# A DiT attention block: the first round of fp32 score products of each step in tiles of 32 rows by 64 columns

## The chip, the core and the metric

The program runs on one core of a Trainium2 chip. The metric is the device time of one execution in microseconds (us), as a median of several runs. Lower is better.

## The reference

One transformer block with adaptive layer norms, in fp32: x is 2 x 2048 x 576, there are 16 heads of 36 features, and every weight and product is fp32.

```python
qkv = (xn @ w_qkv + b_qkv).reshape(B, N, 3, H, hd)
q, k, v = (qkv[:, :, 0], qkv[:, :, 1], qkv[:, :, 2])
q = _ln(q, 1e-05, qn_g, qn_b)
k = _ln(k, 1e-05, kn_g, kn_b)
attn = jnp.einsum('bqhd,bkhd->bhqk', q, k) * scale
attn = jax.nn.softmax(attn, axis=-1)
o = jnp.einsum('bhqk,bkhd->bqhd', attn, v).reshape(B, N, C)
```

Ahead of it stand the modulated layer norm of x, behind it the output projection, a residual, a second norm and a GELU MLP of width 2304. The change touches only the line with `q, k`.

## The kernel before

The block is worked batch by batch: rows are normed and multiplied with w_qkv, then `attend` works the attention of the whole batch, then come projection and MLP. All order on TensorE is the order in which the kernel's text issues the products (a manual schedule).

`attend` walks over steps (p, qb, g): a pair of heads p (8 pairs), a block of 512 queries qb (4 blocks), and a quarter g of the keys (4 quarters). That is 128 steps for a batch and 256 in all. A step issues two things to TensorE:

- `scores(p, qb, g)`: two rounds, one for each `k0`. A round fills four PSUM banks, one for each row group of 32 rows: a row group holds one head of the pair and one half of the keys. In each bank stand 128 keys (partitions) by 512 queries. First the 32 main features are multiplied, in fp32, out of `km` and `qm` (four products of 32 rows by 128 columns, one for each row group); then the remaining four features are added out of `ke` and `qe`, as 16 rows of fp32r parts (again four products, at 128 columns). ScalarE then takes the exponential of each bank into a `pt` tile (L1540).
- `values` of the step before (L1549): the exponentials, 128 rows, against 64 columns of `vt`, in two column tiles, one for each head of the pair, which stand in the two halves of one bank. Four `pt` tiles and two heads make eight products.

So TensorE goes in each step from 32-row tiles of 128 columns (scores) to 128-row tiles of 64 columns (values) and back. The kernel has eight banks; a step takes nine of them in turn (eight for scores, one for values). Every product reads its stationary operand by a weight load (shown as PEld) and then streams 512 columns. An fp32 product is shown as two loads and two matmuls, an fp32r product as one of each.

Two other places come up in the prediction. L178 multiplies the modulation's rows in four column tiles of 32 columns, at 128 rows and then at 64. L1714 and L1717 are the output projection, in tiles of 64 rows and of 128 rows by 128 columns.

Of the kernel before, what the change touches and what calls it, by code (L numbers as in the profile page):

```python
# [16 lines left out]
P = 128  # L17
# [10 lines left out]
DIMS = 32  # L28
# [3 lines left out]
def dit_block(  # L32
# [25 lines left out]
    nc = tc.nc  # L58
    B, N, C = x.shape
    MLP = w1.shape[1]  # L60
    HD = qn_g.shape[0]
# [32 lines left out]
    def bank():  # L94

        return psum["b"].tile([P, 512], F32, tag="b", name="b") if "b" in psum else s_tile()[:, 0, :]
# [650 lines left out]
    def head_rows(first, count=HD):  # L747

        at = first
        while at < first + count:  # L750
            n = min(P - at % P, first + count - at)
            yield at // P, at % P, at - first, n
            at += n

    def block_of_small():
# [108 lines left out]
        def take_k(p):  # L864
            m, e = km[p % 2], ke[p % 2]
            if p > 2:
                not_sooner(m)
                not_sooner(e)
            src = lambda c: slice(c * N // 2, (c + 1) * N // 2)
            rows_taken(nc.gpsimd, m, e, range(2), C + p * 2 * HD, src, slice(0, N // 2))  # L870
            full = slice(0, P)
            return [
                lambda: scaled(m, m, full, 1),
                lambda: parted(e[:, 0:BLK], full, 1),
                lambda: parted(e[:, BLK:], full, 1),
            ]
# [13 lines left out]
        def take_q(p, qb):  # L890
            i, full = qb % 2, slice(0, P)
            src = lambda c: slice(qb * BLK, (qb + 1) * BLK)
            rows_taken(nc.sync, qm[i], qe[i], range(2), p * 2 * HD, src, slice(0, BLK))
            return [lambda: scaled(qm[i], qm[i], full, 0), lambda: parted(qe[i], full, 0)]
# [623 lines left out]
        def attend(b, pool, hooks, key_rows):  # L1518

            def scores(p, qb, g):
                i, j = p % 2, qb % 2
                pts = []
                for k0 in (2 * g * P, (2 * g + 1) * P):
                    keys = slice(k0, k0 + P)
                    banks = [bank() for _ in range(4)]
                    for k, q, first in (  # L1530
                        (km[i], qm[j], True),
                        (ke[i].bitcast(F32R), qe[j].bitcast(F32R), False),
                    ):
                        for r0, ps in zip(range(0, P, 32), banks):
                            r = slice(r0, r0 + (DIMS if first else 4 * (HD - DIMS)))
                            nc.tensor.matmul(ps, k[r, keys], q[r, :], start=first, stop=not first)  # L1536
                    for c in range(2):
                        pt = pool.tile([P, 2, BLK], F32, name="pt", bufs=5)
                        for h in range(2):
                            nc.scalar.activation(pt[:, h, :], banks[2 * c + h], AF.Exp, scale=SCALE)  # L1540
                        pts.append((pt, k0 // P + c * NT // 2))
                return pts

            def values(p, pts):
                acc = bank()
                for pt, kc in pts:
                    for h in range(2):
                        v0 = (kc * H + 2 * p + h) * HV
                        nc.tensor.matmul(  # L1549
                            acc[64 * h : 64 * h + 64, :],  # L1550
                            vt[:, v0 : v0 + 64],
                            pt[:, h, :],
                            start=pt is pts[0][0],
                            stop=pt is pts[-1][0],
                        )
                return acc

            def finish(p, qb, ot, den=None):


                if den is None:
                    den = pool.tile([P, BLK], F32, name="den")
                for h in range(2):
                    sums = den_dram[b, p, qb, h, :]
                    nc.sync.dma_start(out=sums.unsqueeze(0), in_=ot[64 * h + HD : 64 * h + HD + 1, :])
                    nc.sync.dma_start(out=den[64 * h : 64 * h + 64, :], in_=sums.partition_broadcast(64))

                def divided(c0=0, c1=BLK):
                    part = slice(c0, c1)
                    nc.vector.reciprocal(den[:, part], den[:, part])  # L1570
                    nc.vector.tensor_tensor(ot[:, part], ot[:, part], den[:, part], ALU.mult)
                    cols = slice(qb * BLK + c0, qb * BLK + c1)
                    for h in range(2):
                        for c, row, d, n in head_rows((2 * p + h) * HD):
                            for r in (row,) if c < FULL else (row, row + 64):
                                nc.sync.dma_start(
                                    out=held["qo"][r : r + n, c, cols], in_=ot[64 * h + d : 64 * h + d + n, part]
                                )

                return divided  # L1580

            steps = [(p, qb, g) for p in range(NPAIR) for qb in range(NBLK) for g in range(NG)]


            behind, later = None, [[] for _ in range(13)]
            ended = None
            for p, qb, g in [*steps, (None, None, None)]:
                pts = None if p is None else scores(p, qb, g)
                if (p, qb) == (0, 0) and g < len(key_rows):
                    key_rows[g]()  # L1590
                if g == 0 and (p, qb) != (NPAIR - 1, NBLK - 1):
                    for i, do in enumerate(take_q(*((p, qb + 1) if qb + 1 < NBLK else (p + 1, 0)))):
                        later[1 + i].append(do)
                if g == 1 and qb == 0 and p + 1 < NPAIR:
                    for i, do in enumerate(take_k(p + 1)):
                        later[3 + NG * i].append(do)
                if behind is not None:
                    bp, bqb, bg, bpts = behind
                    acc = values(bp, bpts)
                    if bg == 0:  # L1600
                        last = (bp, bqb) == (NPAIR - 1, NBLK - 1)
                        ot = spare[9][:, :BLK] if last else pool.tile([P, BLK], F32, name="ot", bufs=2)
                        nc.vector.tensor_copy(ot, acc)  # L1603
                    else:
                        nc.vector.tensor_tensor(ot, acc, ot, ALU.add)  # L1605
                    if p is None:
                        ended = finish(bp, bqb, ot, spare[10][:, :BLK])
                    elif bg == NG - 1:
                        later[2 if bp == NPAIR - 1 else 3].append(finish(bp, bqb, ot))
                if (p, qb, g) in hooks:  # L1610
                    due = hooks[p, qb, g]() or []
                    later[1] = due[:1] + later[1]
                    later[2] = due[1:] + later[2]
                later.append([])
                for do in later.pop(0):
                    do()
                behind = (p, qb, g, pts)
            for do in [do for group in later for do in group]:
                do()
            return ended  # L1620
# [445 lines left out]
        banks = stack.enter_context(tc.tile_pool(name="ps_m", bufs=1, space=PSUM, reuse_waits="tile"))  # L2066
# [313 lines left out]
        def combined_blocks(out_m, outs):  # L2380

            one = hs.tile([P, QUARTER], F32, name="one", bufs=2)
            nc.scalar.copy(one, out_m[1])  # L2383
            r = hs.tile([P, 2, HALF], F32, name="r", bufs=9)
            left, right = r[:, :, 0:QUARTER], r[:, :, QUARTER:HALF]
            both = lambda ap: ap.unsqueeze(1).to_broadcast([P, 2, QUARTER])
            tt = nc.vector.tensor_tensor
            tt(left, outs[2, 6], both(one), ALU.add)
            tt(right, outs[5, 7], both(left[:, 1]), ALU.add)
            tt(left[:, 1], right[:, 1], out_m[4], ALU.subtract)  # L2390
            tt(right[:, 1], right[:, 1], out_m[5], ALU.add)
            tt(right[:, 0], right[:, 0], out_m[3], ALU.add)
            return r
# [57 lines left out]
        for i, (n, m) in enumerate(products):  # L2451
# [16 lines left out]
            r = combined_blocks(out_m, outs)  # L2468
# [67 lines left out]
```

## Time and profile before

| what | us |
|---|---|
| time, median of 3 runs | 3060.53 (3060.13 to 3061.5) |
| the profiled execution, from its first to its last instruction (its span, and the only time that the profile gives of it) | 3061.8 |
| TensorE busy | 3039.6 (99%) |
| ScalarE busy | 1493.3 (49%) |
| VectorE busy | 1706.3 (56%) |

Busy time is a union of spans in which some instruction of the engine was under way. Matmuls overlap and their ends are modelled, so TensorE at 99% is not TensorE at its peak: the starts of loads and matmuls tell more than their ends.

### The profile page before, as it was taken

The numbers are of one execution on the slowest core, as the hardware profiler recorded it, in microseconds if no ns is written. First come the engines' busy times: TensorE is split into PE (matmuls) and PEld (weight loads), VectorE is DVE, ScalarE is ACT, GpSimd is POOL, SyncE is SP. The second block draws the span as 40 slices with busy tenths as digits, with TensorE's granted clock in tenths as the row PEclk, the third lists the DMA queues.
The fourth block names the chain that finished last, engine by engine and source line by source line (L and its number), as shares of the span: only waits on it lengthen the run. The fifth ranks groups of instructions, "written<-read, shape, count | busy, mean of one in ns | idle before, by whom it ended". The sixth has DMA issues, their size and how long they took to land.

```text
span 3061.8 us, 51356 instructions
## 1 busy us (share of the span) xinstructions
PE 3039.6 (99%) x19015; PEld 1892.7 (62%) x19015; DVE 1706.3 (56%) x2644; ACT 1493.3 (49%) x2917; POOL 1000.6 (33%) x1263
## 2 busy tenths in 40 slices
PE   8999999999999999999999999999999999999998
PEld 6884333333333688633333333347888888999998
DVE  6773455445553666544434444447666664667666
ACT  2326666666666233466666666643555553000000
POOL 4551100132322445201101111115445544545543
PEclk9999999999999999999999999999999999999999
DMA  5773322333333454412222222236888887855554
GB/s 150 187 147 92 103 69 70 81 92 93 94 87 94 162 129 83 94 46 64 52 55 74 62 67 66 77 97 191 250 239 241 243 243 290 311 190 198 206 188 150
DMA packets 427940, 415.17 MB, mean 136 GB/s; under 512 B 231473, under 2 KB 355921, under 8 KB 419553
## 3 DMA queue, kind: packets, MB, share of 16 engines
q1 hardware_dynamic: 390520, 314.46, 34.4%
q0 software_dynamic: 36848, 97.33, 11.7%
q8 instruction: 153, 2.51, 0.3%
q14 instruction: 107, 0.87, 0.1%
q10 hardware_dynamic: 312, 0.01, 0.0%
HBM read 246.43 MB, written 154.75 MB: 131 GB/s over the span
## 4 chain that ended last, share of the span: by engine, by line
PE 99%; DVE 0%; ACT 0%; issue 0%; POOL 0%; DVEq 0%
PE b L1549 30%; PE b L1536 20%; PE b L2366 12%; PE m L2107 12%; PE s L1141 7%; PE s L1227 5%; PE s L1717 4%; PE m L2121 2%; PE one L2107 2%; PE b L2375 2%; PE s L1143 1%; PE s L1233 1%; PE s L1714 1%; PE b L178 0%; PE s L1229 0%; ACT xnt L398 0%
## 5 line engine op out<-in xcount | busy, mean ns | idle before, releaser
L1540 ACT ACTIVATE pt<-b 128x512 f32<-128x512 f32 x2048 | 1057.2, 610 | 482.6 <-PE b L1549 269.4
L1549 PE MATMUL b<-pt,vt 128*64 128x512 f32 x4096 | 935.0, 599 | 0.0
L1549 PEld LDWEIGHTS b<-pt,vt 128*64 128x64 f32 x4096 | 271.9, 136 | 582.0 <-issue 437.6
L1536 PE MATMUL b<-qm,km 32*128 32x512 f32 x4096 | 563.8, 613 | 0.0
L1605 DVE TENSOR_TENSOR ot<-b,ot 128x512 f32<-128x512 f32 x186 | 128.6, 691 | 546.4 <-PE b L1549 546.4
L1536 PE MATMUL b<-qe,ke 16*128 16x512 f32 x2048 | 420.4, 791 | 0.0
L1536 PEld LDWEIGHTS b<-qm,km 32*128 32x128 f32 x4096 | 190.8, 185 | 270.9 <-ACT pt L1540 211.1
L1141 PE MATMUL s<-wq,xnt 128*128 128x288 f32 x864 | 226.7, 406 | 1.5 <-ACT xnt L398 1.5
L2383 ACT COPY one<-b 128x144 f32<-128x144 f32 x55 | 15.3, 278 | 406.0 <-PE b L2366 406.0
L2107 PE MATMUL m<-xnt,wb 128*128 128x256 f32 x864 | 209.1, 379 | 1.4 <-issue 1.3
L2107 PE MATMUL m<-s,wb 128*128 128x256 f32 x864 | 207.4, 379 | 0.0
L1570 DVE RECIPROCAL den<-den 128x512 f32<-128x512 f32 x62 | 206.8, 3336 | 0.0
L1603 DVE COPY ot<-b 128x512 f32<-128x512 f32 x62 | 42.9, 691 | 259.1 <-PE b L1549 253.8
L1141 PEld LDWEIGHTS s<-wq,xnt 128*128 128x128 f32 x864 | 158.0, 190 | 36.9 <-ACT xnt L398 2.2
L1536 PEld LDWEIGHTS b<-qe,ke 16*128 16x128 f32 x2048 | 107.0, 184 | 113.6 <-issue 112.8
L2107 PEld LDWEIGHTS m<-s,wb 128*128 128x128 f32 x864 | 163.6, 190 | 22.0
L2107 PEld LDWEIGHTS m<-xnt,wb 128*128 128x128 f32 x864 | 159.4, 190 | 21.5 <-issue 1.7
L2145 ACT ACTIVATE cs<-cs,b_sb 128x512 f32<-128x512 f32 x144 | 100.1, 720 | 137.8 <-DVE cs L2140 137.6
L1802 POOL DMA_DIRECT2D spare<-in_x_dram x32 | 17.8, 556 | 451.5 <-DVE met L794 451.5
L2147 POOL TENSOR_TENSOR cs<-cs 128x256 f32<-128x256 f32 x72 | 57.5, 798 | 244.5 <-ACT cs L2145 244.5
L1062 ACT ACTIVATE xnt<-xnt,mod 128x128 f32<-128x128 f32 x244 | 100.1, 482 | 51.1 <-DMA xnt<-turned 51.1
L2134 DVE TENSOR_TENSOR cs<-m,cs 128x512 f32<-128x512 f32 x72 | 49.3, 684 | 118.9 <-PE m L2121 76.0
(374 smaller groups left out, 4590.3 us busy)
## 6 DMA issues: line engine op xcount, KB each, us to landing
operands<-cs SPq DMA_DIRECT2D x70, 896.0 KB
wb<-operands SPq DMA_DIRECT2D x37, 1152.0 KB
operand<-operands SPq DMA_DIRECT2D x19, 1152.0 KB
spare<-in_x_dram POOLq DMA_DIRECT2D x64, 288.0 KB, 3.2
x_dram<-spare POOLq DMA_DIRECT2D x64, 288.0 KB, 2.4
qm<-qk SPq DMA_DIRECT2D x256, 64.0 KB
den<-den_dram SPq DMA_DIRECT2D x124, 128.0 KB
spare<-x_dram POOLq DMA_DIRECT2D x37, 288.0 KB, 3.9
```

What stands on the lines that cost most here:

```text
L1062: nc.scalar.activation(part, part, AF.Identity, **affine(which, k, b))
L1141: nc.tensor.matmul(out_a, full[:, k, :], wq[:, k, f], start=k == 0, stop=False)
L1227: nc.tensor.matmul(out[m], x_[:, k, :], w_(k), start=k == 0, stop=k == 1 and m == 6)
L1536: nc.tensor.matmul(ps, k[r, keys], q[r, :], start=first, stop=not first)
L1540: nc.scalar.activation(pt[:, h, :], banks[2 * c + h], AF.Exp, scale=SCALE)
L1549: nc.tensor.matmul(acc[64 * h : 64 * h + 64, :], vt[:, v0 : v0 + 64], pt[:, h, :], start=pt is pts[0][0], stop=pt is pts[-1][0],)
L1570: nc.vector.reciprocal(den[:, part], den[:, part])
L1605: nc.vector.tensor_tensor(ot, acc, ot, ALU.add)
L1717: nc.tensor.matmul(out[m], x_[m][:, k], factors[m][:, k], start=k == 0 and m not in (3, 4), stop=k == 1 and m not in (2, 7),)
L2107: nc.tensor.matmul(out_m[m], wb[:, f, slot[m], k, :], moving[m](k), start=k == 0 and m in firsts, stop=k == 1 and m in lasts,)
L2145: nc.scalar.activation(part, part, AF.Gelu, bias=b1_sb[:, g : g + 1])
L2366: nc.tensor.matmul(out_m[m], stationary[m][:, c, :], w[:, 7 * c + m - 1, :], start=a == 0 and c == 0, stop=ends and c == FULL - 1 and m no ...
```

## The change

In the first round of each step (`k0 == 2 * g * P`) each fp32 product of 32 rows by 128 columns becomes two of 32 rows by 64 columns: first the lower 64 keys of all four row groups, then the upper 64, into the lower and upper 64 partitions of the same four banks. The four fp32r products of that round and the whole second round stay at 128 columns, and so does everything else.

```diff
                 for k0 in (2 * g * P, (2 * g + 1) * P):
-                    keys = slice(k0, k0 + P)
                     banks = [bank() for _ in range(4)]
                     for k, q, first in (
                         (km[i], qm[j], True),
                         (ke[i].bitcast(F32R), qe[j].bitcast(F32R), False),
                     ):
-                        for r0, ps in zip(range(0, P, 32), banks):
-                            r = slice(r0, r0 + (DIMS if first else 4 * (HD - DIMS)))
-                            nc.tensor.matmul(ps, k[r, keys], q[r, :], start=first, stop=not first)
+                        width = 64 if first and k0 == 2 * g * P else P
+                        for c0 in range(0, P, width):
+                            for r0, ps in zip(range(0, P, 32), banks):
+                                r = slice(r0, r0 + (DIMS if first else 4 * (HD - DIMS)))
+                                nc.tensor.matmul(
+                                    ps[c0 : c0 + width, :],
+                                    k[r, k0 + c0 : k0 + c0 + width],
+                                    q[r, :],
+                                    start=first,
+                                    stop=not first,
+                                )
```

## Rows read from the trace of the kernel before

**Rows 1.** The page: busy time of each engine; granted TensorE clock in 40 slices.

```profile
PE 3039.6 (99%) x19015; PEld 1892.7 (62%) x19015; DVE 1706.3 (56%) x2644; ACT 1493.3 (49%) x2917; POOL 1000.6 (33%) x1263
...
PEclk9999999999999999999999999999999999999999
```

**Rows 2.** The chain of waits that ended last: shares of the span by engine and line.

```profile
PE 99%; DVE 0%; ACT 0%; issue 0%; POOL 0%; DVEq 0%
PE b L1549 30%; PE b L1536 20%; PE b L2366 12%; PE m L2107 12%; PE s L1141 7%; PE s L1227 5%; PE s L1717 4%; PE m L2121 2%; PE one L2107 2%; PE b L2375 2%; PE s L1143 1%; PE s L1233 1%; PE s L1714 1%; PE b L178 0%; PE s L1229 0%; ACT xnt L3
```

**Rows 3.** The page's costliest groups: line, operation, tiles, shape, count, busy, mean ns, idle.

```profile
L1540 ACT ACTIVATE pt<-b 128x512 f32<-128x512 f32 x2048 | 1057.2, 610 | 482.6 <-PE b L1549 269.4
L1549 PE MATMUL b<-pt,vt 128*64 128x512 f32 x4096 | 935.0, 599 | 0.0
...
L1536 PE MATMUL b<-qm,km 32*128 32x512 f32 x4096 | 563.8, 613 | 0.0
...
L1536 PE MATMUL b<-qe,ke 16*128 16x512 f32 x2048 | 420.4, 791 | 0.0
L1536 PEld LDWEIGHTS b<-qm,km 32*128 32x128 f32 x4096 | 190.8, 185 | 270.9 <-ACT pt L1540 211.1
```

**Rows 4.** Timeline of weight loads (PEld) over one step: start, length, operation, count, [idle before].

```profile
1307.79 0.31 PEld L1536 LDWEIGHTS b<-qm,km 32*128 32x128 f32 x8 [0.81 <-ACT pt L1540]
1308.32 0.20 PEld L1536 LDWEIGHTS b<-qe,ke 16*128 16x128 f32 x4 [0.22 <-issue]
1308.75 0.45 PEld L1536 LDWEIGHTS b<-qm,km 32*128 32x128 f32 x8 [0.22 <-issue]
1309.42 0.20 PEld L1536 LDWEIGHTS b<-qe,ke 16*128 16x128 f32 x4 [0.22 <-issue]
1310.19 0.20 PEld L1549 LDWEIGHTS b<-pt,vt 128*64 128x64 f32 x4 [0.56 <-ACT pt L1540]
1310.67 0.14 PEld L1549 LDWEIGHTS b<-pt,vt 128*64 128x64 f32 x2 [0.29 <-issue]
1311.10 0.14 PEld L1549 LDWEIGHTS b<-pt,vt 128*64 128x64 f32 x2 [0.28 <-issue]
...
1312.82 0.14 PEld L1549 LDWEIGHTS b<-pt,vt 128*64 128x64 f32 x2 [0.29 <-issue]
1313.77 0.30 PEld L1536 LDWEIGHTS b<-qm,km 32*128 32x128 f32 x7 [0.81 <-ACT pt L1540]
```

**Rows 5.** Timeline of matmuls (PE) of the same step.

```profile
1307.79 1.14 PE L1536 MATMUL b<-qm,km 32*128 32x512 f32 x8
1308.35 0.82 PE L1536 MATMUL b<-qe,ke 16*128 16x512 f32 x4
1308.99 1.04 PE L1536 MATMUL b<-qm,km 32*128 32x512 f32 x8
```

**Rows 6.** Timeline of the projection, where 128-row tiles become 64-row tiles and back.

```profile
2046.81 0.19 PEld L1717 LDWEIGHTS s<-wp,qo 128*128 128x128 f32 x1
...
2047.38 0.30 PEld L1714 LDWEIGHTS s<-wp,qo 64*128 64x128 f32 x4 [0.39 <-DMA spare<-den_dram]
...
2048.22 0.40 PE L1714 MATMUL s<-wp,qo 64*128 64x288 f32 x1
...
2048.55 0.54 PEld L1717 LDWEIGHTS s<-wp_sums,qo 128*128 128x128 f32 x3 [0.39 <-issue]
```

**Rows 7.** Timeline of weight loads where L178's column tiles stand between steps.

```profile
445.72 0.14 PEld L1549 LDWEIGHTS b<-pt,vt 128*64 128x64 f32 x2 [0.28 <-issue]
446.67 0.16 PEld L178 LDWEIGHTS b<-wa,sil 128*32 128x32 f32 x8 [0.81 <-ACT pt L1540]
...
448.96 0.15 PEld L178 LDWEIGHTS b<-wa,sil 64*32 64x32 f32 x8 [0.52 <-issue]
449.63 0.31 PEld L1536 LDWEIGHTS b<-qm,km 32*128 32x128 f32 x8 [0.52 <-issue]
```

**Rows 8.** Timeline of ScalarE over the step of rows 4.

```profile
1309.25 1.08 ACT L1540 ACTIVATE pt<-b 128x512 f32<-128x512 f32 x2 [0.81 <-PE b L1536]
1311.38 3.05 ACT L1540 ACTIVATE pt<-b 128x512 f32<-128x512 f32 x6 [1.04 <-PE b L1549]
```

## The prediction

> **What bounds the kernel now.** First the page: TensorE is busy 99% of the span at full clock in every slice, the other engines a half or less [rows 1]. The chain of waits that ended last says the same: 99% TensorE, 30% of the span in the value products (L1549) and 20% in the score products (L1536) [rows 2]. Whatever TensorE gains or loses per step goes straight into the time. The groups give the counts: 4096 value matmuls at 16 a step are 256 steps, and of a step's 16 fp32 score matmuls (two to a product) the change concerns eight [rows 3].
>
> Busy time can't tell more, since matmuls overlap. The starts of loads and matmuls can: the load of the next pass is issued when a pass begins [rows 4]. One step, from 1307.79 to 1313.77, takes 5.98 us:
>
> - first round: four row groups at once, first fp32 pass 0.53 (1307.79 to 1308.32), second pass 0.43 (to 1308.75), fp32r pass 0.24 (to 1308.99, where the next round's matmuls begin [rows 5]). In all 1.20.
> - second round: 0.43 to 1309.42, another 0.43 and 0.24, which ends at 1310.09; the values begin at 1310.19, 0.10 later.
> - values: first pass 0.48, then 0.43 each. The last load row is at 1312.82, at the start of the seventh of eight passes; two passes on is 1313.68, and the next step begins at 1313.77, 0.09 later [rows 4].
>
> So two things cost TensorE time beside streaming. One is a border of about 0.09 wherever the shape of the tiles changes. The other is the first weight load behind a border, which nothing hides: 0.53 against 0.43 says 0.10 for 128 columns, 0.48 against 0.43 says 0.05 for 64. Inside a mode loads run ahead under the pass before: the second round's first pass takes 0.43 like any other, though its loads are as wide.
>
> The waits put the load at 1313.77 down to ScalarE [rows 4]. I don't believe that: ScalarE is paced by the values, with two exponentials at 1309.25 and six from 1311.38, and ends at 1314.43 [rows 8]. The banks of the first round are old by then, and the idle time is the same 0.81 at a border where another line follows [rows 7]. It is 0.29 + 0.43 + 0.09: the rest of a pass, a pass, the border.
>
> **What the change does to a step.** It removes four fp32 products of 128 columns and adds eight of 64: eight loads and eight matmuls more on TensorE's queue. It adds no transfer, no semaphore wait that another engine has to serve, no bank, no exponential. The product of the streams is the same array work: four row groups by 128 columns before, four row groups by two column halves after. The terms:
>
> 1. *First load.* Values to first round is a border before and after (128*64 to 32*128, now to 32*64). The load behind it has 64 columns in place of 128: 0.05 in place of 0.10, a gain of 0.05. Bounds: 0.05 and nothing (if the two halves of a row group load one after the other). I take 0.05, since two column tiles of 64 columns load together in the values (first pass 0.48 with four loads under way) [rows 4].
> 2. *Eight tiles in place of four.* Loads of one pass start one behind the other: four of 185 ns each [rows 3] span 0.20 [rows 4], so about 6.5 ns apart. The eighth starts 0.045 behind the first. Before, the fp32r pass could follow row group by row group; behind a border it waits for the last tile. Bounds nothing and 0.05; I take 0.05.
> 3. *A new border.* Before, the fp32r products followed in the same mode, 32 rows by 128 columns. Now they come behind tiles of 32*64. The trace has no border from 32*64 to 32*128. It has one where only the rows change, 128*128 to 64*128 and back: a pass of 288 columns is 0.24 (288/512 of 0.43), the last load at 2046.81 and two passes make 2047.29, and the next tile begins at 2047.38; back, 2048.22 and one pass is 2048.46, next tile 2048.55. Both 0.09 [rows 6]. Where only the columns change, 128*64 to 128*32: 445.72 and two passes of 0.43 is 446.58, next tile 446.67, 0.09 again. Where both change, 64*32 to 32*128: 448.96, two passes of 0.27 (320 columns) and a 0.03 load make 449.53, next tile 449.63, 0.10 [rows 7]. Bounds: nothing (if a border with the same rows were free) and 0.11; I take 0.09, as at both neighbours that change one side only.
> 4. *The fp32r load, uncovered.* Before, these 128-column loads ran under the second fp32 pass (the load at 1308.32 [rows 4]). That cover is gone behind a border: 0.10, as in the first round's first pass. Bounds: nothing if item 3 is nothing, otherwise 0.10 to 0.11.
>
> The second round stays hidden: its loads have the 0.24 of the fp32r pass to run under, and the border from the second round to the values is unchanged.
>
> Sum: -0.05 + 0.05 + 0.09 + 0.10 = +0.19 us a step; a step of 5.98 becomes 6.17. Times 256 steps is 48.6 us. On the profiled execution's span of 3061.8 us that is 3110.4; the median of the runs stands 1.3 below that span, so 3109 us, 1.6% slower.
>
> What gets later in turn: the second round begins 0.19 later in its step, so do its exponentials and the values, and all keep their distances. ScalarE has 4.1 us of exponentials in a step (3.05 + 1.08 [rows 8]) and gets more room. Nothing there takes anything back, and nothing adds.
>
> The Trainium skill, TensorEngine Tiling (Array Packing), section Tiling Modes, Key Properties, states that changing the tiling mode drains the array, and lists 32*64 and 32*128 as different ones. No row here shows that pair; by that rule the sum is 3109 us, and were the pair free, case D below would hold. The rows of the other pairs agree with it, at 0.09.
>
> **The rivals.**
>
> *B, the load does not halve.* If the two halves of a row group load one behind the other, item 1 gives nothing: +0.24 a step, 61 us, 3122 us. Against it: the column tiles of the values. For it: there they stand on all rows, and eight tiles nowhere in this trace.
>
> *C, half the borders.* The step from values to 32*64 keeps the width of 64. If that lets the loads run ahead with no border, 0.09 + 0.10 go from the step's start, and +0.05 + 0.09 + 0.10 come: +0.05 a step, 13 us, 3073 us. Against it: the projection's borders keep the width too and cost 0.09 [rows 6].
>
> *D, faster: a border that keeps one side costs nothing.* This is one mechanism with its place at 32*64 to 32*128: the fp32r loads run ahead under the second pass as before, and only -0.05 and half of item 2 (each row group waits for its own upper half) stay, -0.03 a step, 8 us, 3053 us. If it holds at the values' end too, -0.10 - 0.09 + 0.05 = -0.14 a step, 36 us, 3025 us. It decides from the point where the new border with its load is worth under 0.03 a step. Against it: both kinds of one-sided border in the trace [rows 6, 7]; for it only that neither has tiles of 32 rows on both sides.
>
> *E, the eight tiles do not run at once.* An fp32 product is two passes, so for all first passes to start together TensorE has to take the eighth product's first pass ahead of seven waiting second passes. The trace shows four tiles at once: the first round's eight matmuls are two passes of four, 0.53 and 0.43 [rows 4, 5]. If four is the limit, the upper halves begin with the lower halves' second pass: three passes in place of two, +0.43 more, 0.62 a step, 159 us, 3219 us. If the halves go wholly one behind the other it is four passes, 1.05 a step, 269 us, 3329 us. Against it: neither rows nor columns alone show a limit (four row groups in the scores, four column tiles at L178 [rows 7]). For it: no row has more than four.
>
> The Trainium skill, TensorE: Matmul & The Clock Gate, Part 3, section The mechanism, states that matmuls start and end strictly in order. In strict order even four tiles of two passes would need five passes for what these rows do in two, so the trace speaks against it; for eight tiles it stands on the side of E. The same page, section Measured speedup vs the span model, has sixteen tiles of 32*32 running together, which no row here shows and which speaks against E.
>
> **How the numbers follow.** Chances: the sum 0.66, B 0.05, C 0.08, D 0.06, E 0.15. The sum has three kinds of border row behind it; E is the part that the trace can't show. The prediction is the sum, 3109 us. Its own bounds: item 2 at nothing and the rest as taken, +0.14, 3096; items 3 and 4 at 0.11 each, +0.22, 3117. For 8 in 10 I add C below and B above and leave out D and E (0.21 together): 3070 to 3125. This kernel's measurement tells from no change about 0.2%, 6 us. Slower by more than that: the sum, B, C and E, 0.94. D is split: 0.02 within 0.2%, 0.04 faster.
>
> **What the profile of the changed kernel would show.** Step starts 6.17 apart in place of 5.98. In each step: eight loads of 64 columns at the first round's start, the second pass 0.48 behind the first and not 0.53; then a gap of idle time in the loads of about 0.8 before the four fp32r loads, and these loads start together with their matmuls, where before they ran 0.4 ahead; the second round's matmuls some 0.34 behind them (0.10 + 0.24). The second round, the border to the values, and the values as before. VectorE and ScalarE operations keep their lengths, and TensorE stays at 99% with the chain still on L1536 and L1549, the share of L1536 up.
>
> Wrong it would be if the fp32r loads still start under the second pass (D), if the first passes of the two halves start 0.43 apart or more (E), if the second pass starts 0.53 behind the first (B), or if the step's first load starts under the last value pass (C).

## The result

| what | before, us | after, us |
|---|---|---|
| time, median of 4 runs | 3061.02 (3060.13 to 3062.17) | 3106.82 (3106.49 to 3107.59) |
| span of the profiled execution | 3061.8 | 3105.6 |

The ratio is 1.0148, with a 95% interval of 1.0135 to 1.0161: 1.5% slower, where 3109 us and 1.6% were forecast. The medians differ by 45.8 us, 0.179 us for each of 256 steps. The spans of the two profiled executions differ by 43.8 us, 0.171 a step, and the steps inside the two traces say the same: over the 248 steps of each that lead straight into the next, 5.987 us in the mean before and 6.159 after. The forecast had 0.19. The 2 us between the two differences are no more than the runs of the kernel before differ among themselves (3060.13 to 3062.17).

The page of the kernel after, busy time and clock, and the chain of waits (the scores' line is now L1537, the values' L1556):

```profile
PE 3083.5 (99%) x21063; PEld 1835.5 (59%) x21063; DVE 1707.7 (55%) x2644; ACT 1493.3 (48%) x2917; POOL 1000.0 (32%) x1263
...
PEclk9999999999999999999999999999999999999999
...
PE 98%; DMA 1%; DVE 0%; ACT 0%; issue 0%; POOL 0%; SPq 0%; ACTq 0%; DVEq 0%
```

TensorE has 2048 matmuls and 2048 loads more, as the text of the change says, and is the bound as before [rows 1, 2]. Weight loads are busy for *less* time, 1835.5 against 1892.7 us: the sixteen narrow loads of a first round take 0.23 (below), where eight wide ones took 0.31 [rows 4]. ScalarE and VectorE did not change.

The groups of the score products, one row for each shape, after:

```profile
L1537 PE MATMUL b<-qe,ke 16*128 16x512 f32 x2048 | 335.7, 643 | 0.0
L1537 PE MATMUL b<-qm,km 32*64 32x512 f32 x4096 | 288.5, 613 | 0.1
...
L1537 PE MATMUL b<-qm,km 32*128 32x512 f32 x2048 | 264.4, 587 | 0.0
```

Read by busy time the change looks like a gain: the scores are busy for 888.6 us in all (if added up), where 563.8 and 420.4 made 984.2 [rows 3]. That is the trap of overlapping matmuls. The fp32r rows shrank from 791 to 643 ns in the mean because half of them no longer lie in wait behind the pass before them, and not because anything got faster.

The starts tell the time. The timeline of weight loads over one step, after, to be read against [rows 4]:

```profile
1341.99 0.14 PEld L1556 LDWEIGHTS b<-pt,vt 128*64 128x64 f32 x2 [0.29 <-issue]
1342.94 0.23 PEld L1537 LDWEIGHTS b<-qm,km 32*64 32x64 f32 x16 [0.81 <-ACT pt L1547]
1343.99 0.19 PEld L1537 LDWEIGHTS b<-qe,ke 16*128 16x128 f32 x4 [0.81 <-DVE ot L1612]
1344.10 0.43 PEld L1537 LDWEIGHTS b<-qm,km 32*128 32x128 f32 x8
1344.77 0.19 PEld L1537 LDWEIGHTS b<-qe,ke 16*128 16x128 f32 x4 [0.24 <-issue]
1345.51 0.20 PEld L1556 LDWEIGHTS b<-pt,vt 128*64 128x64 f32 x4 [0.56 <-ACT pt L1547]
...
1349.10 0.23 PEld L1537 LDWEIGHTS b<-qm,km 32*64 32x64 f32 x15 [0.81 <-ACT pt L1547]
```

and of the matmuls, with the second fp32 pass of the first round by itself in the second row (from a narrower window):

```profile
1342.94 1.11 PE L1537 MATMUL b<-qm,km 32*64 32x512 f32 x16
...
1343.42 0.63 PE L1537 MATMUL b<-qm,km 32*64 32x512 f32 x8
...
1343.99 0.51 PE L1537 MATMUL b<-qe,ke 16*128 16x512 f32 x4
1344.33 1.03 PE L1537 MATMUL b<-qm,km 32*128 32x512 f32 x8
```

The reader should see four things. The step is 6.16 long (1342.94 to 1349.10), before 5.98. The fp32r loads, which used to start with the second fp32 pass [rows 4], now stand alone at 1343.99, 0.57 behind the start of that pass, with a new idle time of 0.81 before them: the same 0.81 as at the step's start. Their matmuls start with them and the four last 0.51 in all, so the load is bare; before, the records of these matmuls began early too, but lasted 0.82, in wait behind the second fp32 pass [rows 5]. And the sixteen matmuls of the first round are two passes, the second of which begins at 1343.42 with all eight: eight tiles do run together.

The wait for the fp32r loads is put down to VectorE (`DVE ot`) here. As with ScalarE in [rows 4], that is the semaphore which came last before the load; the VectorE operation began at 1343.06 and took 0.69, so it had ended 0.24 earlier. The idle time is 0.81 whoever is named: in the runs below it bears other names or none, once within one run (the rows of every other step).

### The profile page after: what moved, and what is told of

The parts are those of the page before. It is cut to its first block, busy times and chain, and to the rows that moved or that the text cites. A ratio compares the mean times of both kernels' runs of the same rounds, so it can differ in the third digit from the quotient of the medians.

```text
span 3105.6 us, 55653 instructions
## 1 busy us (share of the span) xinstructions
PE 3083.5 (99%) x21063; PEld 1835.5 (59%) x21063; DVE 1707.7 (55%) x2644; ACT 1493.3 (48%) x2917; POOL 1000.0 (32%) x1263
## 4 chain that ended last, share of the span: by engine, by line
PE 98%; DMA 1%; DVE 0%; ACT 0%; issue 0%; POOL 0%; SPq 0%; ACTq 0%; DVEq 0%
PE b L1556 30%; PE b L1537 21%; PE b L2373 12%; PE m L2114 11%; PE s L1141 7%; PE s L1227 5%; PE s L1724 4%; PE m L2128 2%; PE one L2114 2%; PE b L2382 2%; PE s L1143 1%; PE s L1233 1%; DMA operands<-cs 1%; PE s L1721 1%; DMA wq<-in_w_qkv_dram 0%; PE b L178 0%
## 5 line engine op out<-in xcount | busy, mean ns | idle before, releaser
L1556 PE MATMUL b<-pt,vt 128*64 128x512 f32 x4096 | 935.0, 599 | 0.0
L1556 PEld LDWEIGHTS b<-pt,vt 128*64 128x64 f32 x4096 | 272.0, 137 | 582.3 <-issue 437.5
L1537 PE MATMUL b<-qm,km 32*64 32x512 f32 (+1 forms) x6144 | 552.9, 604 | 0.1
L1537 PE MATMUL b<-qe,ke 16*128 16x512 f32 x2048 | 335.7, 643 | 0.0
L1537 PEld LDWEIGHTS b<-qm,km 32*64 32x64 f32 (+1 forms) x6144 | 161.9, 148 | 216.5 <-ACT pt L1547 204.7
L1537 PEld LDWEIGHTS b<-qe,ke 16*128 16x128 f32 x2048 | 98.8, 182 | 268.2 <-issue 217.9
```

The lines of the kernel that those rows point to most:

```text
L1537: nc.tensor.matmul(ps[c0 : c0 + width, :], k[r, k0 + c0 : k0 + c0 + width], q[r, :], start=first, stop=not first,)
L1556: nc.tensor.matmul(acc[64 * h : 64 * h + 64, :], vt[:, v0 : v0 + 64], pt[:, h, :], start=pt is pts[0][0], stop=pt is pts[-1][0],)
```

## The experiments

The six times are medians of four runs each, beside the kernel before on the same chip.

**The narrow tiles in the second round instead.** If narrow tiles are slow by themselves, it does not matter which round has them. If borders are the price, it does: the first round stands behind a border anyway, the second does not.

```diff
-                        width = 64 if first and k0 == 2 * g * P else P
+                        width = 64 if first and k0 != 2 * g * P else P
```

> The second round's fp32 products in tiles of 32 by 64 columns, the first round's at 128 as before the change. Theory (each change of tile shape costs a border of 0.09 us and leaves the first load behind it bare): two new borders in place of one, in front of and behind the fp32 products; a bare load of 64 columns (0.05), the wait for the last of eight tiles (0.05), a bare load of 128 columns (0.10): 0.09 + 0.05 + 0.05 + 0.09 + 0.10 = 0.38 us a step over the kernel before, some 92 to 97 us, 3155 us. Rival (tiles of 64 columns are slow in themselves, a price per round that has them): as many products are narrow as in the changed kernel, so the same 46 us, 3107 us.

Measured: 3158.65 us, ratio 1.0315 (1.0298 to 1.0332) to the kernel before, 96.8 us above its 3061.90 there, 0.378 us a step. The theory said 0.38. The timeline of loads of this kernel, one step:

```profile
1402.30 0.20 PEld L1537 LDWEIGHTS b<-qe,ke 16*128 16x128 f32 x4 [0.22 <-issue]
1403.07 0.23 PEld L1537 LDWEIGHTS b<-qm,km 32*64 32x64 f32 x16 [0.56 <-issue]
1404.11 0.19 PEld L1537 LDWEIGHTS b<-qe,ke 16*128 16x128 f32 x4 [0.81 <-issue]
1404.55 0.20 PEld L1556 LDWEIGHTS b<-pt,vt 128*64 128x64 f32 x4 [0.25 <-ACT pt L1547]
```

There are now idle times on both sides of the narrow products, 0.56 and 0.81. Before the change the second round's loads began 0.43 behind the fp32r loads of the first (1308.32 to 1308.75 [rows 4]); here they begin 0.77 behind (1402.30 to 1403.07), at the same moment as their matmuls:

```profile
1403.07 1.11 PE L1537 MATMUL b<-qm,km 32*64 32x512 f32 x16
```

As many products are narrow as in the changed kernel, at twice its price. The rival that prices narrow tiles themselves falls.

**Sixteen tiles of 32 columns.** This varies the bare load and the number of tiles, and leaves both borders.

```diff
-                        width = 64 if first and k0 == 2 * g * P else P
+                        width = 32 if first and k0 == 2 * g * P else P
```

> The first round's fp32 products in sixteen tiles of 32 by 32 columns in place of eight of 32 by 64. Theory: border and bare 128-column load stay; the first load is bare for 32 columns (0.027 in place of 0.053); the last of sixteen tiles starts 0.10 behind the first in place of 0.05. Together +0.02 to +0.03 us a step over the changed kernel: 3112 us, 3110 to 3115. Rival (a limit on how many tiles run at once, just not below eight): a third pass, +0.43 us a step, 3215 us or more. Rival (narrow tiles are slow in themselves, more so the narrower): a step that grows by about as much again as from 128 to 64 columns, 3150 us.

Measured: 3116.61 us, 1.0176 (1.0159 to 1.0193), 54.7 us above the kernel before. The changed kernel stands 45.8 above its own, so this is 8.9 us more, 0.035 a step: just above the range that was expected, and far from a third pass. First and second pass of one step:

```profile
1402.31 1.14 PE L1537 MATMUL b<-qm,km 32*32 32x512 f32 x32
...
1402.77 0.69 PE L1537 MATMUL b<-qm,km 32*32 32x512 f32 x16
...
1403.38 0.53 PE L1537 MATMUL b<-qe,ke 16*128 16x512 f32 x4
```

The sixteen second passes begin at 1402.77, 0.46 behind the first sixteen; a pass more is not to be seen, and the loads of both passes start within 0.23 (below). The bare load reads off as the first pass less 0.43: 0.53 at 128 columns [rows 4], 0.48 at 64, about 0.46 at 32, that is 0.10, 0.05 and 0.03. The border is then 1403.38 - 1402.77 - 0.43 = 0.18, of which 0.10 is the spread of sixteen starts (in the trace they are 6.7 ns apart, 15 times): 0.08, about as before.

What exceeds the forecast shows in the fp32r loads. Loads in an early step of this run and in the one above:

```profile
574.00 0.19 PEld L1537 LDWEIGHTS b<-qe,ke 16*128 16x128 f32 x4 [0.84 <-issue]
...
575.53 0.20 PEld L1556 LDWEIGHTS b<-pt,vt 128*64 128x64 f32 x4 [0.56 <-ACT pt L1547]
...
1402.31 0.23 PEld L1537 LDWEIGHTS b<-qm,km 32*32 32x32 f32 x32 [0.81 <-ACT pt L1547]
1403.38 0.22 PEld L1537 LDWEIGHTS b<-qe,ke 16*128 16x128 f32 x4 [0.84 <-issue]
...
1404.94 0.20 PEld L1556 LDWEIGHTS b<-pt,vt 128*64 128x64 f32 x4 [0.57 <-ACT pt L1547]
```

The four loads span 0.19 in the early step and 0.22 in the late one, and the values come 1.53 behind them in the early step (574.00 to 575.53), 1.56 in the late one (1403.38 to 1404.94). Early steps take 6.18, which is 0.03 over the changed kernel's 6.16, as expected; 153 of 247 steps, nearly all of them later ones, take 6.20 to 6.22, and that is the excess. What delays these loads is open; it was not tried further.

**Every other step.**

```diff
-                        width = 64 if first and k0 == 2 * g * P else P
+                        width = 64 if first and k0 == 2 * g * P and g % 2 == 0 else P
```

> The change in every other step only (even quarters of the keys), 128 of 256 steps. Theory (a price of each step, with nothing that takes it back later): half of 45.8 us, 3084 us, and the steps in the trace alternate between 5.98 and 6.155 us. Rival (some of the loss belongs to the whole program, such as instruction fetching for the longer queue or another order of the transfers): not half.

Measured: 3085.29 us, 1.0077 (1.0060 to 1.0094), 23.4 us above the kernel before; half of 45.8 is 22.9. Loads at the starts of four steps in turn, with the fp32r loads of the two narrow ones:

```profile
1404.91 0.23 PEld L1537 LDWEIGHTS b<-qm,km 32*64 32x64 f32 x16 [0.81 <-ACT pt L1547]
1405.95 0.19 PEld L1537 LDWEIGHTS b<-qe,ke 16*128 16x128 f32 x4 [0.81 <-DVE ot L1612]
...
1411.06 0.31 PEld L1537 LDWEIGHTS b<-qm,km 32*128 32x128 f32 x8 [0.81 <-ACT pt L1547]
...
1417.04 0.23 PEld L1537 LDWEIGHTS b<-qm,km 32*64 32x64 f32 x16 [0.81 <-ACT pt L1547]
1418.08 0.19 PEld L1537 LDWEIGHTS b<-qe,ke 16*128 16x128 f32 x4 [0.81 <-issue]
...
1423.19 0.31 PEld L1537 LDWEIGHTS b<-qm,km 32*128 32x128 f32 x8 [0.81 <-ACT pt L1547]
```

A step with narrow tiles takes 6.15, the one behind it 5.98, then 6.15 again. The price is paid in the step that has the border, and nothing gives it back.

**No border inside the scores.** The strongest test is narrow tiles everywhere in the scores. For that the last four features are multiplied in fp32 in these three runs, which makes each of those products two passes and the whole kernel slower, so they are compared with one another. The first is the base, at 128 columns throughout:

```diff
-                        (ke[i].bitcast(F32R), qe[j].bitcast(F32R), False),
+                        (ke[i], qe[j], False),
...
-                        width = 64 if first and k0 == 2 * g * P else P
+                        width = P
```

> A base for the next two runs: all score products at 128 columns as in the kernel before, but the products of the last four features as fp32 (two passes of 0.43 us) in place of fp32r (one of 0.24). By the rows of before each round grows by 0.62, a step by 1.25 us, 319 us in all: 3380 us. Theory and rival expect the same here.

Measured: 3378.26 us (3377.23 to 3378.96), 1.1036 (1.1017 to 1.1054) to the kernel before, 317 us above it where 319 were expected. The first loads of a step, the last ones of its scores, and the first of the values:

```profile
1601.75 0.31 PEld L1537 LDWEIGHTS b<-qm,km 32*128 32x128 f32 x8 [0.81 <-ACT pt L1547]
1602.29 0.20 PEld L1537 LDWEIGHTS b<-qe,ke 16*128 16x128 f32 x4 [0.22 <-issue]
...
1604.44 0.21 PEld L1537 LDWEIGHTS b<-qe,ke 16*128 16x128 f32 x4 [0.23 <-issue]
1605.40 0.20 PEld L1556 LDWEIGHTS b<-pt,vt 128*64 128x64 f32 x4 [0.76 <-ACT pt L1547]
```

Then 64 columns throughout (`width = 64`):

> The same with all score products of both rounds, the fp32 ends too, in tiles of 32 by 64 columns: no border inside a step's scores. Theory (borders and bare loads are the price, not the narrow tiles): against the base the bare load behind the values halves (-0.05 us a step), and the border to the values waits for the last of eight tiles (+0.03): -0.02 to -0.03 us a step, 5 to 8 us faster than the base. Rival (narrow tiles are slow in themselves): twice the loss of the changed kernel or more, 90 us slower than the base.

Measured: 3372.89 us (3372.26 to 3374.83), 1.1019 (1.1001 to 1.1037): 5.4 us *faster* than the base, 0.021 a step. The ranges of the two do not meet. One step of scores of this kernel:

```profile
1605.15 0.23 PEld L1537 LDWEIGHTS b<-qm,km 32*64 32x64 f32 x16 [0.81 <-ACT pt L1547]
1605.63 0.18 PEld L1537 LDWEIGHTS b<-qe,ke 16*64 16x64 f32 x8 [0.25 <-issue]
1606.06 0.18 PEld L1537 LDWEIGHTS b<-qe,ke 16*64 16x64 f32 x8 [0.25 <-issue]
1606.49 0.18 PEld L1537 LDWEIGHTS b<-qm,km 32*64 32x64 f32 x8 [0.25 <-issue]
...
1607.78 0.18 PEld L1537 LDWEIGHTS b<-qe,ke 16*64 16x64 f32 x8 [0.25 <-issue]
1608.77 0.20 PEld L1556 LDWEIGHTS b<-pt,vt 128*64 128x64 f32 x4 [0.81 <-ACT pt L1547]
```

From fp32 main products to the ends and on to the next round every pass takes 0.43 and the loads run ahead: there is no border. The narrow bare load at the step's start gains 0.06 by these rows (0.48 in place of 0.54), the wait for the last of eight tiles ahead of the values takes 0.03 back (0.99 in place of 0.96), and the small gain is what is left. Last, the first round wholly at 64 columns and the second at 128 (`width = 64 if k0 == 2 * g * P else P`):

> The same with the whole first round (fp32 ends too) in tiles of 32 by 64 columns and the whole second round at 128: the new border stands between the rounds, with fp32 products on both sides. Theory: as the change did, -0.05 + 0.05 + 0.09 + 0.10 less the 0.01 that the changed kernel got back in the second round: 0.17 us a step, 44 us slower than the base. Rival (the border of the changed kernel belongs to the step from fp32 to fp32r behind column tiles): about 5 us faster to no change against the base.

Measured: 3427.07 us (3426.54 to 3429.64), 1.1196 (1.1177 to 1.1215): 48.8 us above the base, where 44 were expected, 0.191 a step (0.185 by the mean steps of the two traces, 7.422 and 7.237). The border, from 64 to 128 columns in fp32 on both sides:

```profile
1600.70 0.18 PEld L1537 LDWEIGHTS b<-qe,ke 16*64 16x64 f32 x8 [0.25 <-issue]
1601.13 0.18 PEld L1537 LDWEIGHTS b<-qe,ke 16*64 16x64 f32 x8 [0.25 <-issue]
1602.13 0.31 PEld L1537 LDWEIGHTS b<-qm,km 32*128 32x128 f32 x8 [0.81 <-issue]
1602.66 0.20 PEld L1537 LDWEIGHTS b<-qe,ke 16*128 16x128 f32 x4 [0.23 <-issue]
```

The idle 0.81 and the pass of 0.53 behind it (1602.13 to 1602.66) are here too. The price does not need an fp32r product. Nor does it come from adding into a bank whose halves were written apart, since the second round fills four other banks. No version that beats the kernel before came out of these runs: the gain of 0.021 a step needs narrow tiles in all score products, and there the fp32 ends cost 317 us (3378.26 against 3061.48 for the kernel before on that chip). No run has the fp32r products in narrow tiles.

## Why the prediction was right

**What bounds the kernel.** TensorE did, and every 0.01 us of a step came through 256 times. Half the steps gave half the loss, so nothing took it back.

**Item 1, the first load: right.** The first pass takes 0.48 in place of 0.53. The halves of a row group load together, so case B falls; the three widths make it a rule of this trace: bare loads of 0.10, 0.05 and 0.03 for 128, 64 and 32 columns.

**Item 2, the last of eight: right.** From the second pass's start to the fp32r loads it is 0.57 (1343.42 to 1343.99): 0.43, 0.05, and the border. The prediction's 6.5 ns between starts does not follow from its printed rows (0.20 less 0.185 over three gaps is 5 ns), but the trace bears it out: the last of eight tiles starts 0.046 behind the first, 6.7 ns a tile.

**Item 3, the border: right at 0.09.** It was worked out for a pair of shapes that the trace of before did not have, from pairs that change rows alone or columns alone [rows 6, 7]. The rule of the Trainium skill named in the prediction (TensorEngine Tiling (Array Packing), Tiling Modes, Key Properties), that changing the tiling mode drains the array, agrees: between these two modes too the rows show 0.09. C and D, which had half of the borders or all one-sided ones free, fall: the border in front of the 32*64 tiles stayed, with its 0.81, and so did the new one behind them.

**Item 4, the uncovered load: right.** The second round's matmuls begin 0.34 behind the fp32r loads (1343.99 to 1344.33), 0.24 before.

**Case E fell.** Eight tiles start their first passes together (within 0.05), and so do sixteen (within 0.10), each ahead of waiting second passes of the others: in the compiled program the two load and matmul pairs of a product stand next to each other, product after product. The statement of the Trainium skill that matmuls start and end strictly in order (TensorE: Matmul & The Clock Gate, Part 3, The mechanism), weighed in the prediction, is not what these runs show for fp32 products on separate tiles.

**What was off: 0.19 against 0.171 a step.** In the mean of the 248 steps the first round, up to the second round's first matmul, takes 1.381, before 1.198: it costs 0.183, so the four terms were 0.007 too high together. And the second round got shorter: from its first matmul to the values 1.191, before 1.203. "The second round, the border to the values, and the values as before" was the step that missed, by 0.012; the values stayed, at 3.586 in both. The rows show the four fp32r loads a little closer together behind the new border, 0.19 against 0.20, in both rounds, and the second round keeps that: its four fp32r matmuls start within 0.010, before within 0.024, and in both kernels the values begin 0.72 behind the last of them. With fp32 ends, where the load spans 0.20 on both sides, nothing came back. Why the fp32r tiles start closer behind a border was not tested. That an fp32r product is one load and matmul pair and an fp32 product two would fit it.

## What to carry to other kernels

In this kernel cutting tiles to halve a weight load paid only where the neighbours on TensorE's queue had the same tile shape. Count the borders first, and for each new one add the border (0.09 us here), the load behind it, which nothing covers any more (0.10 for 128 columns), and the wait for the last of the tiles ahead of it (0.05 for eight), before counting the gain (0.05). When the shape that you want to change is flanked by one that you can't, the change belongs on both or on neither: with no border inside the scores the narrow tiles were faster by 0.02 a step, with one they were slower by 0.17 to 0.21, with two by 0.38. And read a kernel of overlapping matmuls by the distances of its load starts; the busy times of the score products and of the weight loads fell here while the time rose.

## What the runs showed of the hardware that was not expected

Sixteen tiles of two passes each start all first passes within about 0.1 us, each past the waiting second passes of the tiles ahead of it. At sixteen tiles most steps lose 0.03 us more on the four fp32r loads behind the border (0.22 from the first to the end of the last, against 0.19), without any wait that the trace names.
